# Norm sums and pair sums handed from the vector engine to accumulating transfers in a convolution-and-attention kernel

## The chip, the cores and the metric

The kernel runs on one core of a Trainium2 chip. The metric is the device time of one execution in microseconds, the median of several runs. The core has a matrix engine (PE; its weight loads are listed apart as PEld), a vector engine (DVE), a scalar engine (ACT), a general engine (POOL, also called GpSimd) and a sync engine (SP) that issues most transfers. Each engine works its own list of instructions in order. Sixteen DMA engines move the data of all queues.

## The reference

Four images of 384 channels and 48 x 48 pixels, all in f32. For each image: a 7 x 7 depthwise convolution with a batch norm folded in; a layer norm of the convolution's result over the channels; a layer norm of x; queries, keys and values from the normed x; the normed convolution is added to the queries; attention with 8 heads of 48 over all 2304 pixels; an output projection; and x added at the end.

```python
local = lax.conv_general_dilated(x, conv_w, (1, 1), 'SAME', ..., feature_group_count=C)
local = local * inv[...] + (bn_beta - bn_mean * inv)[...]
x_norm = _layernorm(x_flat, ln_gamma, ln_beta)
q, k, v = split(x_norm @ qkv_w.T + qkv_b)
q = q + _layernorm(local_flat, ln_gamma, ln_beta)
attn = softmax(einsum('bhnd,bhmd->bhnm', q, k) * hd ** -0.5)
out = einsum('bhnm,bhmd->bhnd', attn, v) @ proj_w.T + proj_b
return x_flat + out
```

## The kernel before

Pixels are worked in groups of 8 image rows: G = 384 pixels, NG = 6 groups an image, NT = 24 groups in all. Channels lie on 128 partitions in CC = 3 chunks. Three engines carry the work side by side: PE does all matrix products, ACT the exponentials, and DVE the convolution, one tap of one chunk an instruction (147 steps a group).

**A layer norm** sums over the three chunks on DVE and over partitions by a matmul with a constant matrix:

```python
    class Norm:
        def __init__(self, src):
            self.src = src
            self.buf = work.tile([P, CC, G], F32, tag="sq", name="sq")      # two buffers
        def add(self, src):
            nc.vector.tensor_add(self.buf[:, 0, :], src[:, 0, :], src[:, 1, :])        # L400
            nc.vector.tensor_add(self.buf[:, 0, :], self.buf[:, 0, :], src[:, 2, :])   # L401
        def sum(self):          self.add(self.src)
        def sum_squares(self):  self.add(self.buf)
        def mean(self, m=None):
            self.m = two_banks()[:, 0, :G] if m is None else m
            nc.tensor.matmul(self.m, lhsT=mean_w, rhs=self.buf[:, 0, :], ...)          # L412
        def mean_kept(self):
            m = ring()[:, 0, :G]
            nc.tensor.matmul(m, lhsT=mean_w, rhs=self.buf[:, 0, :], ...)               # L417
            self.m = self.buf[:, 0, :]
            nc.scalar.copy(self.m, m)                                                  # L419
        def root(self, at=slice(0, G)):                      # three steps on ACT, L435 to L437
            nc.scalar.activation(u, self.m[:, at], AF.Ln, bias=eps)
            nc.scalar.activation(y, u, AF.Exp, scale=-0.5)
            nc.scalar.activation(u, y, AF.Square, scale=0.5**0.5)
        # newton() improves the root on DVE; out(), few_centre() ... are the form for later groups,
        # which sums over partitions by transposes and a transfer through DRAM (parts, four)
```

**The prologue** makes keys, values and queries of the first image from x, group after group, and does the first group's convolution beside it:

```python
    first_sum = first_products()
    m, bank = columns()
    convolve_first(10)
    norm = Norm(xn[0, 1])
    norm.sum()
    norm.mean(bank)
    convolve_first(12)
    key_bias(m); query_bias(m)
    next(making)
    norm.centre(); norm.squares()
    # ... (cut)
    for g in range(1, NG):
        last = g == NG - 1
        making = from_x(0, g)
        both(making)
        norm = Norm(accs[0] if last else xn[0, g + 1])
        norm.sum()
        norm.mean()
        if last:
            added = output_bias()         # 18 matmuls of one column, and a copy on ACT
        convolve_first(4)
        norm.centre(); norm.squares()
        both(making)
        # ... (cut)
    query_end(0)
    nc.vector.tensor_add(pb, pb, added)
    plan(n_first - (each - PE_TAPS))
```

**Attention** of one group t takes NSLOT = 12 slots of two halves; a half is three scores. A pair of heads takes three slots, so a pair ends at slots 0, 3, 6 and 9. Scores go to a ring of two PSUM buffers, sums to two more:

```python
    def score(t, p, kb):
        r = ring()
        # ... 8 matmuls into r (L795)
        nc.scalar.activation(pt, r[:, :, :G], AF.Exp, scale=SCALE)     # L803
        weighing.append((t, p, kb, pt))
        if jobs:
            jobs.popleft()()       # one ACT job behind an exponential
    # weigh() does 8 matmuls from pt and the values into sums (L816), two scores later

    def pair_out():
        nc.scalar.copy(dst[0 : 64 + HA], sums[0 : 64 + HA, 0, :G])               # L702
    def pair_add():
        t, p, sums = ended.pop()
        nc.vector.tensor_add(dst, sums[0 : 64 + HA, 1, :G], dst)                 # L711
        # denominators to DRAM (den); after the fourth pair the tails (ao <- aot) too
```

`divide(t - 1)` in slot 2 of the next group loads den, takes reciprocals on DVE and spreads them. The first norm's slots are 8 and 10 for t = 0 (`mean_kept`, then `root`), and 6 and 9 later.

**The plan** gives each half slot a share of convolution steps, from an estimate of the room DVE has in it (`spare`), so that group t + 1 is convolved when its norm begins:

```python
    def spare(t, s, half):
        time = 3.8 - (0.7 if s % 3 == 0 and half else 0.0)    # 0.7 for the pair's add
        # ... less for norms, divisions
```

From the second image on, the keys and values of an image are made before its attention (points "kv"), and the output projection of the image before runs there; it needs `pb`, the output bias.

Of the kernel before, what the change touches and what calls it, by code (L numbers as in the profile page):

```python
# [15 lines left out]
P = 128  # L16
# [29 lines left out]
def unshifted_pass(  # L46
# [55 lines left out]
    def load_packed(dst, src, queue=nc.sync):  # L102
        for p0, piece in segments(src):
            queue.dma_start(out=dst[p0 : p0 + piece.shape[0]], in_=piece)
# [13 lines left out]
    def load_slab(b, g, parts=1):  # L118
        first, end = max(0, g * RG - PAD), min(H, (g + 1) * RG + PAD)
        t = work.tile([P, CC, (RG + 2 * PAD) * W], F32, tag="slab", name=f"slab{b}_{g}")  # L120

        edges = (first, (g + 1) * RG, end) if parts == 2 else (first, end)
        for a, e in zip(edges, edges[1:]):
            load_packed(t[:, :, (a - first) * W : (e - first) * W], x[b, :, a * W : e * W])
        slabs[b, g] = (t, first, end)


    loads = ExitStack()
# [40 lines left out]
                    )  # L169

    load_by_pair(of_ln, ln_pair, (nc.scalar, nc.gpsimd))
    load_slab(0, 0, parts=2)
    place_x(0, 0)
    nc.gpsimd.tensor_scalar_add(inv, norms[:, 3], BN_EPS)
    nc.gpsimd.tensor_tensor(inv, inv, neg_half, ALU.pow)
# [49 lines left out]
        big.tile([P, CC, C], F32, tag=f"k{NG - 1 - i}", name=f"staged{i}") for i in range(3)  # L225
    ]
    load_packed(staged[2], qkv_wT[:, 2 * C :])
    load_packed(staged[1], qkv_wT[:, C : 2 * C])
    load_packed(staged[0], qkv_wT[:, 0:C])
    for g in range(1, NG):  # L230
# [80 lines left out]
    def spare(t, s, half):  # L311
        b, g = divmod(t, NG)
        first, second = norm_slots(t)
        time = 3.8 - (0.7 if s % 3 == 0 and half else 0.0)
        if b + 1 < B and g >= later(b + 1):
            time -= {(3, 1): 2.3, (4, 1): 2.2, (5, 1): 2.3, (7, 0): 0.4, (8, 0): 2.6}.get(
                (s, half), 0.0
            )
        if g:
            time -= {(2, 0): 0.7, (4, 1): 1.4}.get((s, half), 0.0)  # L320
        if t == 0:
            time -= {(7, 1): 1.1, (8, 1): 1.4, (9, 1): 1.1, (11, 0): 5.0}.get((s, half), 0.0)
        elif t + 1 < NT:
            time -= {(5, 1): 2.3, (6, 1): 2.2, (7, 1): 2.3, (9, 0): 0.4, (10, 0): 4.5}.get(
                (s, half), 0.0
            )
        return max(0.3, time)
# [48 lines left out]
    class Norm:  # L376
# [26 lines left out]
        def sum(self):  # L403
            self.add(self.src)

        def sum_squares(self):
            self.add(self.buf)

# [5 lines left out]
        def mean_kept(self):  # L414

            m = ring()[:, 0, :G]
            nc.tensor.matmul(m, lhsT=mean_w, rhs=self.buf[:, 0, :], start=True, stop=True)  # L417
            self.m = self.buf[:, 0, :]
            nc.scalar.copy(self.m, m)  # L419

        def mean_of(self, src, at):

# [8 lines left out]

        def root(self, at=slice(0, G)):

            y, u = self.buf[:, 1, at], self.buf[:, 2, at]
            nc.scalar.activation(u, self.m[:, at], AF.Ln, bias=eps)  # L435
            nc.scalar.activation(y, u, AF.Exp, scale=-0.5)
            nc.scalar.activation(u, y, AF.Square, scale=0.5**0.5)  # L437

        def newton(self, at=slice(0, G)):

# [138 lines left out]
    def both(making):  # L579
        next(making)  # L580
        next(making)
# [72 lines left out]
    def output_bias():  # L654

        m = ring()[:, 0, 0:CC]
        for co in range(CC):
            project(
                m[:, co : co + 1],
                lambda c: w_o[:, c, co * P : (co + 1) * P],  # L660
                lambda c: vbp[:, c, :],
            )
        added = const.tile([P, CC], F32, tag="inv", name="added")
        nc.scalar.copy(added, m)
        return added


    queries = {}
# [21 lines left out]
    def pair_out():  # L690

        if not ended:
            return
        t, p, sums = ended[0]
        if p == 0:
            ao = work.tile([P, CC, G], F32, tag="ao", name=f"ao{t}")
            ao3 = work.tile([P, G], F32, tag="aot", name=f"aot{t}", bufs=1)
            den = dram.tile([NH, G], F32, tag="den", name=f"den{t}")
            outputs[t] = ao, ao3, den
        ao, ao3, den = outputs[t]  # L700
        dst = ao[:, p, :] if p < CC else ao3
        nc.scalar.copy(dst[0 : 64 + HA], sums[0 : 64 + HA, 0, :G])  # L702

    def pair_add():

        if not ended:
            return
        t, p, sums = ended.pop()
        ao, ao3, den = outputs[t]
        dst = (ao[:, p, :] if p < CC else ao3)[0 : 64 + HA]  # L710
        nc.vector.tensor_add(dst, sums[0 : 64 + HA, 1, :G], dst)  # L711
        for j in range(2):
            r = 64 * j
            nc.sync.dma_start(out=den[2 * p + j : 2 * p + j + 1], in_=dst[r + HD : r + HA])
        if p == NP - 1:
            for c in range(CC):
                for r in (0, 64):
                    nc.sync.dma_start(
                        out=ao[r + HD : r + 64, c, :], in_=ao3[r + 16 * c : r + 16 * c + 16]
                    )  # L720
# [105 lines left out]
    def attend(t, s, half):  # L826
# [3 lines left out]
        for kb in range(k0 + n * half, k0 + n * half + n):  # L830
            score(t, p, kb)
            if len(weighing) > LAG:
                weigh()

    def rest():
        while weighing:
            weigh()
        while jobs:
            jobs.popleft()()

# [4 lines left out]
    def convolve_first(n):  # L847
        nonlocal n_first
        n_first += n
        for _ in range(n):  # L850
            next(stream)
# [40 lines left out]
    m, bank = columns()  # L892
    convolve_first(10)
    norm = Norm(xn[0, 1])
    norm.sum()
    norm.mean(bank)
    convolve_first(12)
    key_bias(m)
    query_bias(m)
    next(making)  # L900
    norm.centre()
    norm.squares()
    both(making)
    convolve_first(2)
    add_products()
# [8 lines left out]
    for g in range(1, NG):  # L914

        last = g == NG - 1
        making = from_x(0, g)
        both(making)
        assert not last or n_first >= each - PE_TAPS
        norm = Norm(accs[0] if last else xn[0, g + 1])  # L920
        norm.sum()
        norm.mean()
        if last:
            added = output_bias()
        convolve_first(4)
        norm.centre()
        norm.squares()
        both(making)
        if not last:
            convolve_first(4)  # L930
            both(making)
        norm.sum_squares()
        norm.mean()
        norm.root()
# [3 lines that stand above are left out]
        convolve_first(6 if last else 10)  # L938
        if last:
            local_end(0, norm.newton())  # L940
        else:
            norm.scale(norm.newton())
        both(making)
        if not last:
            convolve_first(7)
    query_end(0)
    nc.vector.tensor_add(pb, pb, added)
    plan(n_first - (each - PE_TAPS))

    for t in range(NT):  # L950
        b, g = divmod(t, NG)
        if g == 0 and b:

            rest()
            pair_out()
            pair_add()
            load_x(b, NG - 1)
            norms_x = {}
            for gk in range(NG):
                before = t - NG + gk  # L960
                load_residual(before)
                making = from_x(b, gk, before, ao if gk < NG - 1 else outputs[before][0])
                new = NG - later(b) + gk if gk < later(b) else None
                old = norms_x.get(gk - 1)
                both(making)
                convolve("kv", t, gk, 0)
                if new is not None:
                    norms_x[gk] = Norm(xn[b, new])
                    norms_x[gk].sum()
                    norms_x[gk].out()  # L970
                both(making)
                if old:
                    old.few_variance()
                    old.few_root()
                if gk == 1:
                    query_end(t)
                    rb = divide(t - 1)
                if gk == 2:
                    last_ao = outputs[t - 1][0]
                    nc.vector.tensor_mul(last_ao, last_ao, rb)  # L980
                convolve("kv", t, gk, 1)
                both(making)
                convolve("kv", t, gk, 2)
                if new is not None:
                    norms_x[gk].few_centre()
                    norms_x[gk].squares()
                both(making)
                convolve("kv", t, gk, 3)
                if old:
                    old.scale(old.few_newton())  # L990
                both(making)
                convolve("kv", t, gk, 4)
                if new is not None:
                    norms_x[gk].sum_squares()
                    norms_x[gk].out()
                both(making)
                if gk < NG - 2:
                    ao = fetch(before + 1)
# [4 lines left out]
        for s in range(NSLOT):  # L1003
# [39 lines left out]
            if coming and s == X_SLOTS[1]:  # L1043
                norm_x.few_root()
            if following and s == second:
                norm.few_root() if t else norm.root()
            if s == first and t == 0:
                norm.centre()
            convolve("slot", t, s, 1)
# [585 lines left out]
```

## Time and profile before

| | |
|---|---|
| time, median of 3 runs | 2857.66 us (2856.81 to 2859.96) |
| profiled span | 2857.6 us |
| prologue | to about 144 us, where the first scores start |
| first image's attention | to about 719 us |
| convolution steps (line 284) | 3447, mean 582 ns by their own records |
| exponentials (line 803) | 1728, 810 ns |
| score matmuls (line 795) and weighing matmuls (line 816) | 13824 each, 8 of each a step |
| pair copies on ACT (line 702), pair adds on DVE (line 711) | 0.47 us, 0.55 us |

In the profile, "L284" is a line of the kernel; a row of the groups or of the order of time names the engine, the operation, what it writes and reads (out<-in), the shapes and how many instructions are merged in it. A bracket at its end tells how long the engine stood idle before it, and what ended that. Durations of overlapping instructions run into each other, so a run of n merged instructions gives a better mean than one record.

### The profile page before, as it was taken

The page shows a single profiled execution, that of the slowest core. Times are in us where ns is not written, and L with a number is a line of the kernel's source. Part 1 is how long each engine was busy: PE and PEld are TensorE (multiplying, and loading weights), DVE is VectorE, ACT ScalarE, POOL GpSimd, SP SyncE. Part 2 cuts the span into 40 slices and gives each one's busy share as a digit, 9 for nine tenths or more (in the row PEclk, how much of TensorE's full clock was granted, in tenths as well). Part 3 has the DMA queues.
Part 4 walks back from the last instruction along what each step waited for, and adds up shares of the span by engine and source line. Part 5 has one row for each costly group of instructions (what it writes and reads, how often), then busy time and mean ns, then how long its engine had stood idle before and what let it go on. Part 6 is the DMA issues. An engine that isn't in the chain of part 4 may idle for free.

```text
span 2857.6 us, 70328 instructions
## 1 busy us (share of the span) xinstructions
PE 2838.7 (99%) x29558; PEld 1778.1 (62%) x29558; DVE 2344.6 (82%) x4635; ACT 1649.5 (58%) x2350; POOL 14.9 (1%) x77
## 2 busy tenths in 40 slices
PE   9999999999999999999999999999999999999999
PEld 5544444654554466666655546888875545788886
DVE  7899999999888988878888889887788787887401
ACT  4366666666226666666622666666652366666662
POOL 1000000000000000000000000000000000000000
PEclk9999999999999999999999999999999999999999
DMA  5101121112231211121132112101113211111111
GB/s 106 40 5 36 45 49 35 36 26 43 71 83 25 46 35 41 31 39 24 38 94 70 28 30 50 36 22 37 44 25 94 53 20 29 43 23 32 46 38 63
DMA packets 103433, 123.71 MB, mean 43 GB/s; under 512 B 43136, under 2 KB 89152, under 8 KB 103104
## 3 DMA queue, kind: packets, MB, share of 16 engines
q1 hardware_dynamic: 99568, 115.48, 17.0%
q8 instruction: 234, 3.83, 0.6%
q10 hardware_dynamic: 2992, 3.62, 0.4%
q14 instruction: 95, 0.78, 0.1%
q0 software_dynamic: 544, 0.01, 0.0%
HBM read 81.39 MB, written 27.03 MB: 38 GB/s over the span
## 4 chain that ended last, share of the span: by engine, by line
PE 92%; DVE 6%; DMA 0%; POOL 0%; ACT 0%; issue 0%; DVEq 0%; ACTq 0%; POOLq 0%
PE o L816 37%; PE r L795 37%; PE o L503 9%; PE r L503 9%; DVE acc L284 5%; DMA pb<-in_proj_b_dram 0%; PE r L299 0%; PE r L412 0%; ACT pt L803 0%; DVE sq L401 0%; DVE xn L681 0%; DMA parts<-part 0%; DVE sq L400 0%; POOL qk_vec L167 0%; DVE acc L672 0%
## 5 line engine op out<-in xcount | busy, mean ns | idle before, releaser
L803 ACT ACTIVATE pt<-r 128x768 f32<-128x768 f32 x1728 | 1399.6, 810 | 760.1 <-PE r L795 743.6
L284 DVE SCALAR_TENSOR_TENSOR acc<-slab,vec,acc 128x368 f32<-128x368 f32 (+6 forms) x3447 | 1756.3, 582 | 1.2
L816 PE MATMUL o<-pt,v 64*64 64x384 f32 x13824 | 1544.7, 483 | 0.0
L795 PE MATMUL r<-xn,k 48*64 48x384 f32 x10368 | 1157.8, 483 | 3.7 <-ACT pt L803 3.7
L816 PEld LDWEIGHTS o<-pt,v 64*64 64x64 f32 x13824 | 715.3, 133 | 406.7 <-issue 224.0
L795 PEld LDWEIGHTS r<-xn,k 48*64 48x64 f32 x10368 | 531.9, 133 | 316.2 <-issue 176.1
L795 PE MATMUL r<-qt,kt 48*64 48x384 f32 x3456 | 388.1, 482 | 0.1
L795 PEld LDWEIGHTS r<-qt,kt 48*64 48x64 f32 x3456 | 181.3, 133 | 99.1 <-issue 43.8
L711 DVE TENSOR_TENSOR ao<-o,ao 113x384 f32<-113x384 f32 x72 | 39.9, 554 | 194.0 <-PE r L795 176.8
L503 PE MATMUL o<-xn,w_qk 128*128 128x384 f32 x450 | 153.3, 486 | 0.0
L503 PE MATMUL r<-xn,w_qk 128*128 128x384 f32 x414 | 141.1, 486 | 0.0
L503 PEld LDWEIGHTS o<-xn,w_qk 128*128 128x128 f32 x450 | 85.5, 190 | 59.6
L503 PEld LDWEIGHTS r<-xn,w_qk 128*128 128x128 f32 x414 | 78.7, 190 | 54.8
L536 ACT COPY v<-r 128x384 f32<-128x384 f32 x42 | 18.2, 482 | 126.9 <-PE r L503 126.9
L503 PE MATMUL r<-w_v,xn 128*128 128x384 f32 x252 | 85.2, 487 | 0.0
L711 DVE TENSOR_TENSOR aot<-o,aot 113x384 f32<-113x384 f32 x24 | 13.3, 556 | 82.4 <-ACT aot L702 64.8
L503 PE MATMUL o<-af,w_o 128*128 128x384 f32 x222 | 75.0, 487 | 0.0
L400 DVE TENSOR_TENSOR sq<-sq 128x384 f32<-128x384 f32 x47 | 26.0, 554 | 57.7 <-ACT sq L395 56.2
L503 PEld LDWEIGHTS r<-w_v,xn 128*128 128x128 f32 x252 | 47.6, 190 | 34.4 <-issue 1.8
L503 PE MATMUL o<-w_v,xn 128*128 128x384 f32 x180 | 64.4, 498 | 1.3 <-ACT w_v L635 1.3
L503 PEld LDWEIGHTS o<-af,w_o 128*128 128x128 f32 x222 | 42.1, 190 | 29.2
L771 DVE SCALAR_TENSOR_TENSOR xr<-r,pb,xr 128x384 f32<-128x384 f32 x27 | 16.4, 617 | 51.8 <-ACT xn L555 41.9
(139 smaller groups left out, 1036.9 us busy)
## 6 DMA issues: line engine op xcount, KB each, us to landing
xr<-in_x_dram SPq DMA_DIRECT2D x24, 576.0 KB
slab<-in_x_dram SPq DMA_DIRECT2D x32, 378.0 KB
held<-ao SPq DMA_DIRECT2D x20, 576.0 KB
af<-held SPq DMA_DIRECT2D x20, 576.0 KB
rb<-rden SPq DMA_DIRECT2D x48, 216.0 KB
out_dram<-xr SPq DMA_DIRECT2D x54, 192.0 KB
xn<-in_x_dram SPq DMA_DIRECT2D x46, 216.0 KB
slab<-in_x_dram SPq DMA_DIRECT2D x14, 297.0 KB
```

The lines of the kernel that those rows point to most:

```text
L284: nc.vector.scalar_tensor_tensor(dst, src, weight, dst, ALU.mult, ALU.add)
L400: nc.vector.tensor_add(self.buf[:, 0, :], src[:, 0, :], src[:, 1, :])
L503: nc.tensor.matmul(dst, lhsT=weights(c), rhs=src(c), start=c == 0, stop=c == CC - 1)
L536: nc.scalar.copy(v[:, blk, :, 0:HD], r[:, :C].rearrange("p (h d) -> p h d", d=HD))
L711: nc.vector.tensor_add(dst, sums[0 : 64 + HA, 1, :G], dst)
L771: nc.vector.scalar_tensor_tensor(xr[:, co, :], m, pb[:, co : co + 1], xr[:, co, :], ALU.add, ALU.add)
L795: nc.tensor.matmul(r[h, j, :G], lhsT=kk[:, blk * P + h.start : blk * P + h.stop], rhs=qq, start=True, stop=True,)
L803: nc.scalar.activation(pt, r[:, :, :G], AF.Exp, scale=SCALE)
L816: nc.tensor.matmul(sums[halves[j], i, :G], lhsT=values[t // NG, kb // NB][h, first : first + 64], rhs=pt[h, j, :], start=kb == 0, stop=kb ...
```

## The change

It takes work off DVE beside the first image. Sums of x over the chunks (groups 1 to 5) are made by three transfers that GpSimd issues: one copy, and two that add to what is there. The two halves of a pair's sums are added in the same way: ACT copies the second half too, and a transfer adds it. The room so made is given to the convolution, in the prologue (14 for 12, 6 for 4 steps) and in the plan. The output bias moves from the last prologue group to the start of the second image. The copy of the first kept mean and the root's three steps become jobs that run one at a time behind exponentials. The first slab's lower rows are loaded after the value weights instead of before them.

```diff
@@ load_slab: two parts, the second loaded by a call
-    load_slab(0, 0, parts=2)
+    rest_of_slab = load_slab(0, 0, parts=2)
@@
     load_packed(staged[2], qkv_wT[:, 2 * C :])
+    rest_of_slab()
     load_packed(staged[1], qkv_wT[:, C : 2 * C])
@@ spare
-        time = 3.8 - (0.7 if s % 3 == 0 and half else 0.0)
+        time = 3.8 - (0.7 if s % 3 == 0 and half and t > NG else 0.0)
@@ Norm
+        def sum_by_transfers(self):
+            nc.gpsimd.dma_start(out=self.buf[:, 0, :], in_=self.src[:, 0, :])
+            for c in (1, 2):
+                nc.gpsimd.dma_start(
+                    out=self.buf[:, 0, :], in_=self.src[:, c, :], accum_op=ALU.add
+                )
@@ mean_kept
-            nc.scalar.copy(self.m, m)
+            jobs.append(lambda: nc.scalar.copy(self.m, m))
@@ root, as three steps that can be queued
+        def root_jobs(self, at=slice(0, G)):
+            y, u, m = self.buf[:, 1, at], self.buf[:, 2, at], self.m[:, at]
+            yield lambda: nc.scalar.activation(u, m, AF.Ln, bias=eps)
+            yield lambda: nc.scalar.activation(y, u, AF.Exp, scale=-0.5)
+            yield lambda: nc.scalar.activation(u, y, AF.Square, scale=0.5**0.5)
@@ output_bias
-        return added
+        nc.vector.tensor_add(pb, pb, added)
@@ pair_out
+        if t < NG:
+            other = work.tile([P, G], F32, tag="other", name="other", bufs=1)
+            def other_half():
+                nc.scalar.copy(other[0 : 64 + HA], sums[0 : 64 + HA, 1, :G])
+                nc.gpsimd.dma_start(
+                    out=dst[0 : 64 + HA], in_=other[0 : 64 + HA], accum_op=ALU.add
+                )
+            jobs.append(other_half)
@@ pair_add
+        all_jobs()
-        nc.vector.tensor_add(dst, sums[0 : 64 + HA, 1, :G], dst)
+        if t >= NG:
+            nc.vector.tensor_add(dst, sums[0 : 64 + HA, 1, :G], dst)
@@ prologue
     norm = Norm(xn[0, 1])
-    norm.sum()
+    norm.sum_by_transfers()
     norm.mean(bank)
-    convolve_first(12)
+    convolve_first(14)
@@
     norm.squares()
+    norm_next = Norm(xn[0, 2])
+    norm_next.sum_by_transfers()
@@ for g in range(1, NG)
-        norm = Norm(accs[0] if last else xn[0, g + 1])
-        norm.sum()
+        if last:
+            norm = Norm(accs[0])
+            norm.sum()
+        else:
+            norm = norm_next
         norm.mean()
-        if last:
-            added = output_bias()
-        convolve_first(4)
+        convolve_first(4 if last else 6)
         norm.centre()
         norm.squares()
+        if g + 2 < NG:
+            norm_next = Norm(xn[0, g + 2])
+            norm_next.sum_by_transfers()
@@
-    nc.vector.tensor_add(pb, pb, added)
@@ start of a later image
+            if b == 1:
+                output_bias()
@@ slots
-                norm.few_root() if t else norm.root()
+                norm.few_root() if t else jobs.extend(norm.root_jobs())
```

More of the change, by code (lines that the diff above doesn't have):

```diff
@@ L120, in load_slab, with load @@
         t = work.tile([P, CC, (RG + 2 * PAD) * W], F32, tag="slab", name=f"slab{b}_{g}")
-        edges = (first, (g + 1) * RG, end) if parts == 2 else (first, end)
-        for a, e in zip(edges, edges[1:]):
+        slabs[b, g] = (t, first, end)
+        def load(a, e):
             load_packed(t[:, :, (a - first) * W : (e - first) * W], x[b, :, a * W : e * W])
-        slabs[b, g] = (t, first, end)
+        if parts == 1:
+            load(first, end)
+        else:
+            load(first, (g + 1) * RG)
+            return lambda: load((g + 1) * RG, end)
     loads = ExitStack()
@@ L432, in root @@
         def root(self, at=slice(0, G)):
[L434 to L437, printed above, removed]
+            for step in self.root_jobs(at):
+                step()
+        def root_jobs(self, at=slice(0, G)):
[3 more added lines that the diff above has]
+            yield lambda: nc.scalar.activation(u, y, AF.Square, scale=0.5**0.5)
         def newton(self, at=slice(0, G)):
@@ L833, in attend, with all_jobs @@
                 weigh()
+    def all_jobs():
+        while jobs:
+            jobs.popleft()()
     def rest():
@@ L837, in rest @@
             weigh()
-        while jobs:
-            jobs.popleft()()
+        all_jobs()
     stream = chain(*(conv_ops(t) for t in range(NT)))
@@ L919, in unshifted_pass @@
         assert not last or n_first >= each - PE_TAPS
-        norm = Norm(accs[0] if last else xn[0, g + 1])
-        norm.sum()
+        if last:
+            norm = Norm(accs[0])
+            norm.sum()
+        else:
+            norm = norm_next
         norm.mean()
-        if last:
-            added = output_bias()
-        convolve_first(4)
+        convolve_first(4 if last else 6)
         norm.centre()
         norm.squares()
+        if g + 2 < NG:
+            norm_next = Norm(xn[0, g + 2])
+            norm_next.sum_by_transfers()
         both(making)
```

## The prediction

> **What bounds the kernel now.** I read the page's busy table first, then PE's own waits, then the table by stage over the first image, then order of time around each gap. The chain by line and the slices added nothing the stages do not show better.
>
> ```profile
> PE 2838.7 (99%) x29558; PEld 1778.1 (62%) x29558; DVE 2344.6 (82%) x4635; ACT 1649.5 (58%) x2350; POOL 14.9 (1%) x77
> ```
>
> PE is busy 2838.7 of 2857.6 us, so all its idle time together is 18.9 us, 0.7% of the span. No change that leaves the matmuls alone can win 2%. What PE waits for, in the view of PE's waits (us in total, times, longest):
>
> ```profile
> PE r L417 <- DVE sq L401: 3.9, 1, 3.9
> PE r L795 <- ACT pt L803: 3.7, 5, 2.6
> ...
> PE r L412 <- DVE sq L401: 1.5, 2, 0.9
> ```
>
> Three gaps after the start-up: one where the mean matmul of the second group's convolution (line 417) waits for a VectorE sum, one where a score waits for an exponential, one at a norm's mean (line 412). The table by stage (length, then busy time of PE, PEld, DVE, ACT, POOL, clock, DMA) says who is behind them:
>
> ```profile
> 150.00:200.00 50.00, 50.00 (x624) 23.47 (x620) 50.00 (x98) 32.03 (x41) 0.00 (x0) 1.00 0.01 2
> 200.00:400.00 200.00, 193.44 (x2312) 92.67 (x2308) 198.00 (x385) 124.62 (x166) 0.00 (x0) 0.97 0.19 43
> ```
>
> Beside the first image DVE is full (50.00 of 50, 198 of 200). ACT has room, POOL does nothing. In order of time around the first gap:
>
> ```profile
> 200.77 11.76 DVE L284 SCALAR_TENSOR_TENSOR acc<-slab,vec,acc 128x368 f32<-128x368 f32 x23
> ...
> 212.45 0.54 DVE L400 TENSOR_TENSOR sq<-acc 128x384 f32<-128x384 f32 x1
> ...
> 213.03 0.56 DVE L401 TENSOR_TENSOR sq<-sq,acc 128x384 f32<-128x384 f32 x1
> ...
> 213.73 1.62 PE L417 MATMUL r<-sq,mean_w 128*128 128x384 f32 x2 [3.93 <-DVE sq L401]
> ...
> 219.18 1.33 PE L816 MATMUL o<-pt,v 64*64 64x384 f32 x8
> ...
> 220.33 0.82 PE L795 MATMUL r<-xn,k 48*64 48x384 f32 x8
> ```
>
> DVE comes 3.93 us late. The gap costs more than itself: groups of eight matmuls start 1.28 us apart until about 220.3, 0.65 after. From 213.73 to 220.33 PE does the mean and four groups, 0.32 + 4 x 0.65 = 2.9 us at full pace, in 6.6: another 3.7. So **gap A is worth 7.6 us**. **Gap B** at 311 us:
>
> ```profile
> 311.07 0.88 PE L795 MATMUL r<-xn,k 48*64 48x384 f32 x8 [2.55 <-ACT pt L803]
> ```
>
> ACT waited for squares whose centring on DVE ended at 309.77; six groups then take 5.62 us instead of 3.88. Worth 2.55 + 1.74 = 4.3. **Gap C** at 125.6 us: 0.92 of wait, then 18 one-column matmuls of the output bias, then six matmuls in 3.45 us instead of 1.94. Worth 0.9 + 1.5 = 2.4. A + B + C = 14.3 us: all three gone would give 2843.4.
>
> **What the Trainium skill says.** "TensorE: Matmul & The Clock Gate", Part 1, says the PE clock halves after an idle window of about 3.4 us and returns after as long a busy one. The trace agrees: the 1.28 and 0.65 us above, and a granted clock of 0.86 in the stretch 200 to 225. "DMA: Bandwidth & Descriptors", SWDGE vs HWDGE vs iDMA, and its Rules for kernel authors: accumulating is for GpSimd-issued transfers alone, and an accumulate must wait for the completion of an earlier transfer to the same bytes. Its Anatomy of one DMA gives about 2.0 us fixed plus bytes / 436 GB/s; for 128 x 384 f32, 197 kB, that is an estimate of 2.45 us each. No accumulate is in this trace, but its GpSimd-issued loads took longer, and much longer while the start-up loads run:
>
> ```profile
> qk_vec<-in_qk_b_dram POOLq DMA_DIRECT2D x2, 1.1 KB, 3.2
> ...
> pb<-in_proj_b_dram POOLq DMA_DIRECT2D x1, 1.5 KB, 7.0
> ```
>
> **The change, part by part.**
>
> *1. Sums of x by transfers.* Five norm sums, two DVE adds each (0.55 + 0.56), leave DVE: 5 x 1.11 = 5.6 us. In exchange 2 + 4 x 2 = 10 more convolution steps are done in the prologue, 10 x 0.52 = 5.2 (the x23 row: 11.76 / 23 = 0.51). DVE's prologue stays as long, but it enters the first image with 20 steps done instead of 10. For groups 2 to 5 the three transfers have a whole group, 18.7 us, to land: hidden. The first does not. Its load is issued from 13.9 us; by the GB/s of the slices up to 60 us about 3.0 MB have moved by 19.5 us and this tile's last byte is near 3.1 MB, so it lands at about 21.5. Its mean is needed when PE reaches it:
>
> ```profile
> 33.46 0.91 PE L412 MATMUL r<-sq,mean_w 128*128 128x384 f32 x2
> ```
>
> That leaves 12 us for three serial transfers. At 4 us each (an estimate: 3.2 measured on small ones and 0.5 to 1 for the bytes) they end at 33.5: no loss. At 7.0 as the pb load had them while all 16 DMA engines were full (DMA stays full to about 38 us), they end at 42.5: PE waits 9 us, and some 1.7 of slow clock follow. PE and DVE both stand, so it is lost whole. I choose +4 as the middle.
>
> *2. Output bias moved to the second image.* 18 matmuls in 2.32 us leave gap C and come back later: zero by themselves. The slow 1.5 us after them should go; some of the 0.9 may. PE then gets to the mean of the squares earlier, and DVE's 2.45 us wait for the root at 136.7 closes. -2.
>
> *3. Pair halves by copy and transfer.* Four DVE adds a group leave, 4 x 0.55 = 2.2 us, 24 x 0.554 = 13.3 us in the image. ACT gets 24 copies of 0.47, each behind an exponential, in a pause of 0.48: they fit. The transfer itself is read only by the reciprocals: copies at 250.5 and about 252, transfer 4 to 256, denominators 2, then SP issues six tail transfers in 3.7 and the reload of den at about 262, landing near 265. The reciprocal ran at 267.12 and DVE will be some us earlier: 0 to 2 us of DVE wait per group, 0 on PE.
>
> *4. The plan.* Working the plan's formula through with the new room: up to the point before the mean of gap A 131 steps instead of 137, and up to slot 6 of the second group 274 instead of 284. **Gap A**: DVE saves 6 x 0.52 + 2 x 0.54 + 0.1 = 4.3 us there; part 2 makes PE about 1.4 us more early than DVE. Lateness 3.93 + 1.4 - 4.3 = about 1 us, too short for the clock to fall. -7.6 + 1 = -6.6. **Gap B**: between A and B DVE saves 4 more steps and 4 adds, 4.2, but PE comes 3.7 earlier because the slow clock of A is gone, and part 5 costs DVE some 2.5. It stays about as it is: 0.
>
> *5. Steps behind exponentials.* The kept mean takes one of two ring buffers. Its copy moves from straight after the mean to after the next exponential (233.38 mean, next exponential 235.22 to 236.03): the second score, which started at 235.57 and takes the buffer the mean had, now starts at about 236.55. 1 us, at slots 8 and 10: +2. The root's three steps (0.61, 0.53, 0.52) now end near 243.0, after the third exponential of slot 11, instead of 240.24. DVE stood 0.60 for them and will stand up to 3.
>
> *6. Rest of the first slab behind the value weights.* Weights come about 1.2 us earlier (216 kB at 180 GB/s), but PE then waits for the last weights at 19.75 anyway, whose place in the queue is unchanged: 0.
>
> Sum: +4 - 2 - 6.6 + 0 + 2 + 0 = -2.6; 2857.66 - 2.6 = 2855.1. Since parts 1 and 5 are costs that I inferred and part 4 is a gain that the trace shows directly, I lean a little towards the gain: **2854.5 us**.
>
> **The rivals.** *The first sum becomes the new wait.* For it: three dependent transfers, full DMA engines, 7.0 us for 1.5 KB, PE in order. Against: a packet of another queue need not wait behind all that is outstanding; 3.2 was measured at 8 us. With 10.7 in place of 4: about 2861. *The start is hidden and gap B closes too.* For it: DVE loses 13.3 us of adds in an image where it is full; against: the faster PE eats it between A and B. Then -2 - 6.6 - 4.3 + 2: about 2847. *Transfers of 113 rows are slow*, the denominators come late and DVE stalls in each of five groups. For it: 113 rows do not divide over 16 engines. Against: the 12 to 15 us that lie between. At 5 us more each, DVE falls behind PE again and gap A's saving is lost at B: about 2863.
>
> **Range and chances.** The two outcomes of part 1 lie near 2848 and 2860, with a few us of spread from B and C on each side; the three runs of before spread by 3. Eight in ten: 2845 to 2866. A gain of 2% needs 57 us where 18.9 exist; a loss of 2% needs a repeated stall nowhere seen. Faster 0.005, within 2% 0.985, slower 0.01.
>
> **What would show it.** Part 1: PE's wait before the mean at about 33 us, named for a transfer into sq; 0 to 1 us says hidden, over 5 says the rival. Parts 3 and 4: no wait over 1.5 us at the kept mean near 210, clock 1.00 there, DVE adds of ao only from the second image on. B: a wait of some 2 to 3 us for an exponential near 300; none says DVE gained more than I think. Part 5: two gaps of about 1 us before the second score after each kept mean. Part 2: no slow matmuls at 128, perhaps some near 715. Wrong outright would be waits in later images, where DVE has slack.

## The result, and the profile after

The changed kernel takes 2870.15 us (median of 4 runs, 2869.6 to 2871.37) against 2858.14 us of the kernel before in the same comparison: a ratio of 1.0042, 95% interval 1.0025 to 1.006. It is 12 us slower, and outside the predicted range of 2845 to 2866.

The busy table of the kernel after:

```profile
PE 2837.4 (99%) x29558; PEld 1872.0 (65%) x29558; DVE 2328.5 (81%) x4601; ACT 1658.9 (58%) x2374; POOL 46.4 (2%) x116
```

DVE lost 16 us of work, as meant, and PE does the same matmuls. But PE's idle time rose from 18.9 us to 2869.5 - 2837.4 = 32.1. PE's waits of the kernel after (us in total, times, longest) say where:

```profile
PE r L427 <- DMA sq<-xn: 14.4, 1, 14.4
PE r L828 <- ACT pt L836: 5.2, 7, 3.4
...
PE r L427 <- DVE sq L408: 0.5, 1, 0.5
```

The 3.9 us for the first kept mean's sum is gone. In its place stands one wait of 14.4 us for a transfer into sq: the chain of three transfers that makes the first sum. The wait for an exponential has grown from 2.6 to 3.4. The stages of the kernel after, in the columns shown before:

```profile
0.00:50.00 50.00, 31.37 (x161) 22.86 (x162) 21.87 (x65) 19.84 (x61) 15.74 (x46) 0.88 0.98 162
...
150.00:200.00 50.00, 49.71 (x550) 24.83 (x552) 49.93 (x96) 30.32 (x41) 0.88 (x1) 1.00 0.06 10
200.00:400.00 200.00, 195.72 (x2360) 96.65 (x2355) 195.51 (x379) 129.56 (x177) 6.67 (x8) 0.98 0.23 47
```

In the first 50 us PE is busy for 31.37 (44.99 before), and the DMA engines are busy for 98% of the stretch. From 200 to 400 us PE is busy 2.3 us longer than before, in spite of its wait at 318 us. The chain itself, in the kernel after's order of time from 18 us on:

```profile
23.69 0.55 POOL L415 DMA_DIRECT2D sq<-xn  x1 [9.53 <-DMA xn<-in_x_dram]
...
31.75 0.91 POOL L417 DMA_DIRECT2D sq<-xn  x1 [7.51 <-DMA sq<-xn]
...
38.87 0.87 POOL L417 DMA_DIRECT2D sq<-xn  x1 [6.20 <-DMA sq<-xn]
...
48.15 1.65 PE L427 MATMUL r<-sq,mean_w 128*128 128x384 f32 x2 [14.42 <-DMA sq<-xn]
...
49.83 0.16 DVE L670 TENSOR_TENSOR qkb<-qk_vec,r 128x3 f32<-128x3 f32 x1 [15.98 <-PE r L427]
```

Each bracket names what the engine waited for: in the first row GpSimd (POOL) waits for the load of x, in the next two for its own transfer before. The three take about 8, 7 and 9 us, one after the other; PE reaches the mean at 33.7 us, 0.3 later than before, and stands until 48.15. DVE stands 15.98 us with it, so nothing is done in that time that was saved elsewhere. Later sums run the same three transfers in 3.0 us each (a median). The transfers into sq in the stretches 20 to 50 us and 50 to 140 us (count, KB each, median us to landing):

```profile
sq<-xn POOLq DMA_DIRECT2D x5, 192.0 KB, 7.8
```

```profile
sq<-xn POOLq DMA_DIRECT2D x10, 192.0 KB, 3.0
```

The two gaps of the first image, in the kernel after's order of time:

```profile
221.54 0.85 PE L849 MATMUL o<-pt,v 64*64 64x384 f32 x8
222.32 0.91 PE L432 MATMUL r<-sq,mean_w 128*128 128x384 f32 x2
223.16 0.88 PE L828 MATMUL r<-xn,k 48*64 48x384 f32 x8
223.86 0.83 PE L849 MATMUL o<-pt,v 64*64 64x384 f32 x8
225.03 0.88 PE L828 MATMUL r<-xn,k 48*64 48x384 f32 x8 [0.34 <-ACT pt L836]
...
318.63 1.56 PE L828 MATMUL r<-xn,k 48*64 48x384 f32 x8 [3.39 <-ACT pt L836]
```

Gap A is closed: the mean follows the matmuls before it and the clock stays full. The score at 225.03 comes 1.17 us after the group before it, not 0.65. It takes the buffer that the mean had, and the copy out of that buffer now stands behind an exponential (224.16 us) and starts at 224.87. Gap B is wider. Six points that both profiles have, as starts of the same instruction, make a ledger:

| point | before | after | difference | step |
|---|---|---|---|---|
| first mean of the prologue | 33.46 | 48.15 | +14.7 | |
| second mean | 38.80 | 54.38 | +15.6 | +0.9: 1.45 of slow clock after the wait, less a wait of 0.56 that is gone |
| first score | 144.35 | 156.93 | +12.6 | -3.0, of which 2.3 is the bias, moved |
| second kept mean (slot 10) | 233.38 | 239.41 | +6.0 | -6.6, gap A |
| first score of the second group's last pair | 320.57 | 329.33 | +8.8 | +2.7, gap B |
| first score of the second image | 857.82 | 868.52 | +10.7 | +1.9, the bias |

From there to the last matmul the difference stays 10.7; the last 1.2 of the span's 11.9 come behind it, in the last output transfers, which the change doesn't touch.

### The profile page after: what moved, and what is told of

Its sections match the earlier page's. It is cut to its first block, busy times and chain, and to the rows that moved or that the text cites. A ratio compares the mean times of both kernels' runs of the same rounds, so it can differ in the third digit from the quotient of the medians.

```text
span 2869.5 us, 70442 instructions
## 1 busy us (share of the span) xinstructions
PE 2837.4 (99%) x29558; PEld 1872.0 (65%) x29558; DVE 2328.5 (81%) x4601; ACT 1658.9 (58%) x2374; POOL 46.4 (2%) x116
## 3 DMA queue, kind: packets, MB, share of 16 engines
q10 hardware_dynamic: 2992, 3.62, 0.4%
## 4 chain that ended last, share of the span: by engine, by line
PE 94%; DVE 4%; DMA 1%; issue 1%; ACT 0%; SPq 0%; POOL 0%; DVEq 0%; POOLq 0%; ACTq 0%
PE r L828 38%; PE o L849 38%; PE o L522 9%; PE r L522 9%; DVE acc L291 3%; DMA staged<-in_qkv_wT_dram 0%; DMA sq<-xn 0%; DMA xn<-in_x_dram 0%; ACT pt L836 0%; PE r L427 0%; DVE xn L517 0%; DMA parts<-part 0%; DMA slab<-in_x_dram 0%; DVE xn L443 0%; DVE sq L461 0%
## 5 line engine op out<-in xcount | busy, mean ns | idle before, releaser
L849 PE MATMUL o<-pt,v 64*64 64x384 f32 x13824 | 1575.9, 483 | 0.0
L828 PE MATMUL r<-xn,k 48*64 48x384 f32 x10368 | 1179.9, 483 | 5.1 <-ACT pt L836 4.9
L849 PEld LDWEIGHTS o<-pt,v 64*64 64x64 f32 x13824 | 763.8, 133 | 359.3 <-issue 143.6
L828 PEld LDWEIGHTS r<-xn,k 48*64 48x64 f32 x10368 | 566.6, 133 | 282.9 <-issue 111.0
L828 PE MATMUL r<-qt,kt 48*64 48x384 f32 x3456 | 397.1, 482 | 0.3 <-ACT pt L836 0.3
L828 PEld LDWEIGHTS r<-qt,kt 48*64 48x64 f32 x3456 | 194.4, 133 | 86.8 <-issue 29.1
L744 DVE TENSOR_TENSOR ao<-o,ao 113x384 f32<-113x384 f32 x54 | 30.0, 556 | 194.7 <-PE r L828 176.6
```

The lines of the kernel that those rows point to most:

```text
L828: nc.tensor.matmul(r[h, j, :G], lhsT=kk[:, blk * P + h.start : blk * P + h.stop], rhs=qq, start=True, stop=True,)
L849: nc.tensor.matmul(sums[halves[j], i, :G], lhsT=values[t // NG, kb // NB][h, first : first + 64], rhs=pt[h, j, :], start=kb == 0, stop=kb ...
```

## The experiments

My theory: the chain of the first sum costs the 15.6 us, because the DMA engines are full of start-up loads; without it the change is a gain. The rivals: something else would make PE wait there anyway; an accumulating transfer is slow at the start by itself; and what the deferred copies win or lose was open. Every time below is a median beside runs of the kernel before on the same chip.

**The first sum on DVE again**, all else as changed:

```diff
     norm = Norm(xn[0, 1])
-    norm.sum_by_transfers()
+    norm.sum()
     norm.mean(bank)
```

> The changed kernel with the sum of group 1 alone made by two vector adds again, all else as changed. Theory (the three chained transfers of the first sum, beside the start-up loads, cost the 14.4 us wait and about 1 us of slow clock after it): the wait at the first mean goes to 0 to 1 us and the time falls by 14 to 16 us to 2854 to 2857. Rival (the transfers only show a wait that something else, such as the later arrival of loads, would bring anyway): the wait stays above 5 us and the time above 2861.

Measured: 2855.05 us, ratio 0.9988 (0.9981 to 0.9995). PE's wait for a transfer into sq is gone from its list; the first score starts at 141.50 us. The one line turns a loss of 12 us into a gain of 3.5. **The chain alone**, in the kernel before:

```diff
     norm = Norm(xn[0, 1])
-    norm.sum()
+    norm.sum_by_transfers()
     norm.mean(bank)
```

> The kernel before with the sum of group 1 alone made by three transfers, and nothing else of the change. Theory: the same wait of 13 to 16 us appears before the first mean, and the time rises by 13 to 17 us to 2871 to 2875. Rival (the wait needs the other parts, such as the next group's transfers that go out behind the third one, or the moved slab rows): a wait under 8 us and a time under 2867.

Measured: 2875.08 us, ratio 1.0053 (1.0036 to 1.007), 16.5 us over the kernel before, at the upper end of what was expected. PE's waits in it:

```profile
PE r L420 <- DMA sq<-xn: 14.0, 1, 14.0
PE r L425 <- DVE sq L401: 3.9, 1, 3.9
```

The same wait without any other part of the change, and gap A still there. So the chain is cause enough, both ways.

**Why it is slow.** All else as changed, but the loads that stand behind x's group 1 are issued later, by ACT, group by group:

```diff
-    for g in range(1, NG):
-        load_x(0, g)
+    load_x(0, 1)
-    load_packed(w_o, proj_wT)
@@ prologue
+    load_x(0, 2, nc.scalar)
     first_sum = first_products()
@@ after norm.squares()
+    load_x(0, 3, nc.scalar)
@@ in the loop over g, after norm.squares(): load_x(0, g + 3), the second slab at g == 1, w_o at g == 3
```

> The changed kernel with the loads of x of groups 2 to 5, of the second slab and of the projection weights issued later, by ACT, one group at a time, so that the three transfers of the first sum run while little else moves. Theory (each transfer is slow because the DMA engines are full of loads): each takes 3 to 4 us instead of 7 to 9, the wait at the first mean falls to 0 to 2 us, the time to 2854 to 2859. Rival (an accumulating transfer is slow at the start by itself, or GpSimd is slow to issue it): each still takes 6 us or more, and the wait stays above 7 us.

Measured: 2856.14 us, ratio 0.999 (0.9983 to 0.9996). The order of time of this kernel:

```profile
22.52 0.55 POOL L415 DMA_DIRECT2D sq<-xn  x1 [9.01 <-DMA xn<-in_x_dram]
...
27.04 0.91 POOL L417 DMA_DIRECT2D sq<-xn  x1 [3.97 <-DMA sq<-xn]
...
32.16 0.87 POOL L417 DMA_DIRECT2D sq<-xn  x1 [4.21 <-DMA sq<-xn]
...
35.30 1.65 PE L427 MATMUL r<-sq,mean_w 128*128 128x384 f32 x2 [2.06 <-DMA sq<-xn]
```

4.5, 5.1 and 3.1 us instead of 8, 7 and 9, with the same instructions at the same place. While these three run, the DMA engines are busy for 0.55, 0.71 and 0.55 of the time; in the changed kernel for 0.99 or more. The first two missed the 3 to 4 us expected: a load of 1.2 MB for residuals (SP at 16.5 us) and the next group's (ACT at 26.4 us) still run beside them. The wait falls from 14.4 to 2.06. It is the load on the DMA engines; neither the accumulate nor GpSimd's issue is slow by itself. Nor does DVE's work hold GpSimd up: in the changed kernel the third transfer took 9.28 us while DVE stood still.

**Copy and root straight in ACT's order**, all else as changed:

```diff
-            jobs.append(lambda: nc.scalar.copy(self.m, m))
+            nc.scalar.copy(self.m, m)
@@
-                norm.few_root() if t else jobs.extend(norm.root_jobs())
+                norm.few_root() if t else norm.root()
```

> The changed kernel with the copy of the kept mean and the three root steps straight in ACT's order again instead of behind exponentials. Theory (the copy behind an exponential holds one of two ring buffers and makes a gap of about 1.1 us twice): both gaps go, and 2 to 4 us are won, 2866 to 2868. Rival (the jobs shield PE from ACT, as they were meant to): no gain, or up to 3 us more.

Measured: 2865.05 us, ratio 1.0024 (1.0016 to 1.0033), 5 us under the changed kernel. That is more than expected, but not all of it belongs to the edit: in this profile the first mean waits 12.4 us, 2 less than in the changed kernel, since x's group 1 landed 1.7 us earlier. From the first score on (154.62) to the second group's last pair (321.19) it takes 166.6 us, against 172.4 in the changed kernel: the edit is worth 5.8 us there. Gap B went from 3.39 us to 1.68, and the slow clock behind it is gone (six groups took 6.81 us from 318.63 in the changed kernel, 3.88 at full pace: 2.9 of the 5.8):

```profile
313.37 0.88 PE L828 MATMUL r<-xn,k 48*64 48x384 f32 x8 [1.68 <-ACT pt L836]
```

**Both remedies together**, and the first sum made by PE, which needs no vector work at all:

```diff
     norm = Norm(xn[0, 1])
-    norm.sum_by_transfers()
-    norm.mean(bank)
+    norm.m = bank
+    project(bank, lambda c: mean_w, lambda c: norm.src[:, c, :])
```

> The changed kernel with the sum of group 1 made by PE (three accumulating matmuls into the mean instead of one) and the kept mean's copy and the root straight in ACT's order. Theory (the first sum costs some 15 us, the two deferrals some 5 us, and the two add up): 2849 to 2852, a ratio to the kernel before of 0.997 to 0.998. Rival (the direct copies won only because they took time out of what the long wait had shifted): no better than the kernel with the sum on the vector engine alone, 2854 to 2856.

Measured: 2851.48 us, ratio 0.9975 (0.9965 to 0.9984). The profiled span is 2848.6. This beats both kernels, the one before by 7 to 8 us. What PE waits for in it between 150 and 860 us is one row:

```profile
PE r L828 <- ACT pt L836: 2.0, 2, 1.7
```

From this kernel I took single parts out again. **Which of the two deferrals** costs: the root deferred alone, then the copies alone.

```diff
-                norm.few_root() if t else norm.root()
+                norm.few_root() if t else jobs.extend(norm.root_jobs())
```

> The kernel with the sum on PE and the kept mean's copy direct, but the root's three steps behind exponentials as in the change. Theory (the later root makes the vector engine stand about 2.6 us for it, and what it loses comes out at the gap near 300 us): that wait grows from 1.7 to 3 us or more, with slow clock after it, and the time is 2 to 4 us above the kernel with both direct. Rival (the whole loss of the deferrals is the mean's copy): within 1 us of it.

Measured: 2855.8 us, ratio 0.9991 (0.9983 to 0.9999). DVE's and PE's rows in the order of time:

```profile
234.38 0.62 DVE L461 SCALAR_TENSOR_TENSOR sq<-sq,eps 128x384 f32<-128x384 f32 x1 [1.45 <-ACT sq L456]
```

```profile
303.73 0.88 PE L828 MATMUL r<-xn,k 48*64 48x384 f32 x8 [3.62 <-ACT pt L836]
```

Without the deferral DVE's step starts at 232.16 us, with no wait. With 1.45 us of standing at 234, gap B at 304 grows from 1.68 to 3.62 us. From the first score to the second group's last pair it takes 2.0 us more than with both direct (168.55 for 166.54); no slow clock followed this time. The median is 4.3 us higher; what this profile has beyond the 2.0 lies elsewhere (its scores start 0.7 us later, and 1.7 us of slow matmuls come at 711 us), and is not shown to be the edit's.

```diff
-            nc.scalar.copy(self.m, m)
+            jobs.append(lambda: nc.scalar.copy(self.m, m))
```

> The kernel with the sum on PE and the root direct, but the copies of the kept mean behind an exponential as in the change. Theory (each copy holds one of the two ring buffers for one exponential longer): two gaps of about 1.1 us at slots 8 and 10 of the first group, the time about 2 us above the kernel with both direct, the gap near 300 us at about 1 us or less because PE comes later to it. Rival (the copy is harmless): within 1 us and no gaps.

Measured: 2852.62 us, ratio 0.9978 (0.9969 to 0.9988), not to be told from the kernel with both direct. Its gaps are there, half as long as expected, and gap B is shorter for them:

```profile
210.47 0.88 PE L828 MATMUL r<-xn,k 48*64 48x384 f32 x8 [0.34 <-ACT pt L836]
...
227.57 0.88 PE L828 MATMUL r<-qt,kt 48*64 48x384 f32 x8 [0.34 <-ACT pt L836]
...
301.60 0.88 PE L828 MATMUL r<-xn,k 48*64 48x384 f32 x8 [1.03 <-ACT pt L836]
```

By the same two points it takes 0.5 us more (167.03). So of the two the root is the costly one; with the slow clock that such a gap B can bring, the parts make up 5.4 of the 5.8: 2.0 + 0.5 + 2.9. **The pair halves on DVE again:**

```diff
-        time = 3.8 - (0.7 if s % 3 == 0 and half and t > NG else 0.0)
+        time = 3.8 - (0.7 if s % 3 == 0 and half else 0.0)
@@ pair_out
-        if t < NG:
+        if t < 0:
@@ pair_add
-        if t >= NG:
+        if t >= 0:
```

> The same, and the pair halves of the first image added by the vector engine again, with the plan's room as before. It tells what the pair transfers bring. Theory (the 13 us of vector work they take away matter only up to the gaps near 205 and 300 us, where the vector engine is late): PE waits 1 to 3 us longer there, the time is 2 to 5 us more than without this edit. Rival (the ten convolution steps done in the prologue are enough by themselves): within 1 us of it.

Measured: 2854.59 us, ratio 0.9985 (0.9978 to 0.9991). Gap B is 3.2 us, and 0.3 us of wait stand at the second kept mean (225.09 us); gap A stays closed. From PE's waits and from the order of time:

```profile
PE r L432 <- DVE sq L408: 0.3, 1, 0.3
```

```profile
303.38 0.88 PE L828 MATMUL r<-xn,k 48*64 48x384 f32 x8 [3.20 <-ACT pt L836]
```

The pair transfers bring about 3 us. **The sums of groups 2 to 5 on DVE again**, with 12 and 4 steps in the prologue:

```diff
-    convolve_first(14)
+    convolve_first(12)
@@
-            norm = norm_next
+        norm = Norm(accs[0] if last else xn[0, g + 1])
+        norm.sum()
@@
-        convolve_first(4 if last else 6)
+        convolve_first(4)
@@ norm_next and the calls that start its transfers are gone
```

> The kernel with the sum of group 1 on PE and the direct copies, and the sums of groups 2 to 5 by vector adds as before, with 12 and 4 convolution steps in the prologue as before. It tells what the hidden transfers of sums bring. Theory (ten steps fewer are done when the first image starts, 5 us of vector work): a wait of 1 to 4 us comes back at the kept mean near 205 us or the one near 300 grows, and the time is 2 to 6 us more. Rival (the pair transfers alone are enough): within 1 us.

Measured: 2858.58 us, ratio 1.0 (0.9992 to 1.0009). Gap A is back, with its slow clock:

```profile
211.93 1.62 PE L432 MATMUL r<-sq,mean_w 128*128 128x384 f32 x2 [2.95 <-DVE sq L408]
```

The hidden sums by transfer, with the ten steps they make room for, bring about 7 us, more than expected and more than the pairs. With the 3 us of the pairs that is more than the whole gain over the kernel before, so the two are not a sum; a kernel without both was not run. Last, **more of the same**, 8 steps for 6 in each of four prologue groups:

```diff
-        convolve_first(4 if last else 6)
+        convolve_first(4 if last else 8)
```

> The kernel with the sum on PE and the direct copies, and 8 instead of 6 convolution steps in each of the four prologue groups, so 8 steps (4.2 us of vector work) fewer are left for the first image. Theory (the gap near 300 us comes from a vector engine that is late by 2 us or so): that wait goes from about 1.7 us to under 0.5 and 1 to 3 us are won, 2847 to 2850. Rival (the vector engine is full in the prologue too): PE waits there by as much, and nothing is won.

Measured: 2851.87 us, ratio 0.9974 (0.9966 to 0.9983): nothing won. Gap B is gone (0.3 us is all PE waits for an exponential from 150 to 860 us), but the first score starts at 144.34 us instead of 142.31. The rival holds: DVE is full in the prologue too, and what gap B gave the prologue took.

## Why the prediction was wrong, step by step

**Part 1 failed, by the size that I chose.** "I choose +4 as the middle" between 0 and 10.7; measured +15.6 (14.4 of wait, 0.3 of shift, and 0.9 that the slow clock cost beyond a wait of 0.56 that went away). Three terms were off, all one way. The tile was used from 23.69 us on, not 21.5. The transfers took 8, 7 and 9 us instead of 7.0 each at most, since they lengthen the load they stand in: before, the DMA engines were full to about 38 us; in the kernel after, to about 47. And the argument against, that "a packet of another queue need not wait behind all that is outstanding", did not help: the first transfer landed by 31.75 us, with the engines full to about 47, but sharing them was slow enough; with the load taken away the same three took 12.8 us instead of 24.5. I had a measured 7.0 us for a transfer of 1.5 KB (issued at 12.15 us) beside the same start-up loads and set an estimate of 4 from idle engines beside it as equally likely. With the 7.0 believed, the rival's number, 2861, would have been the prediction, and still 9 us short.

**Part 1's other half was right**: in the loop the sums are hidden (no PE wait for one), and ten steps enter the first image early. Taking it out cost 7 us.

**Part 2** was close: -3.0 at the first score and +1.9 in the second image are -1.1 where I had -2; a wait of 1.0 us at 146.4 for an ACT copy took its place. The slow clock after the bias matmuls went from 128 us; see below for where it can come back.

**Part 3** was right: the copies fit behind exponentials (0.47 us, no wait of PE named for them), and up to 860 us DVE waited for the reloaded denominators once, 1.5 us. The rival of slow 113-row transfers has nothing for it.

**Part 4** was right on gap A: it closed, -6.6 predicted, -6.6 measured. That the figures agree is luck. From the group before the mean to the fifth group behind it the kernel before takes 11.36 us (208.97 to 220.33), the kernel after 4.83 (221.54 to 226.37), of which 0.52 are a gap of part 5: so gap A was worth 7.05, not 7.6 (mean and next start are 0.84 apart at full pace, where I had put 0.32). DVE came in time, where I had left 1 us of lateness, and the 0.52 made up the rest. On gap B it was not: 0 predicted, +2.7 with the second such gap in it, so +2.2. Gap B is now worth 3.39 + 2.93 = 6.3 us, against 4.3: the wait is 0.8 longer, where I had the root's 2.5 us of DVE (2.64 measured, at 249.50) balanced by other savings, and 1.2 more is slow clock, which I had left at its old size.

**Part 5** had the right mechanism for the copies at twice the size: 1.17 - 0.65 = 0.52 us each, +1.0 instead of +2. The root's delay to DVE, which the same part names, is what gap B shows. The score starts at 225.03, while the copy's record runs from 224.87 to 225.34; why it can start before that ends was not tried.

**Part 6** was right: the weights are used earlier and PE waits longer for the last ones (1.85 us for 0.93), to 19.95 us where it was 19.75.

Sum by the ledger: +15.6 - 1.1 - 6.6 + 2.7 = +10.6, and 1.2 behind the last matmul: 11.8 of the 12.0. The kernel with the first sum on PE and the direct copies shows what the rest of the reasoning was worth: 2851.5, with gap A closed and gap B at 1.7.

## What to carry to other kernels

A transfer takes longer in company: the same 192 KB took 7 to 9 us beside the start-up loads and 3.0 later. Before handing a sum on the critical path to transfers, take its latency from rows of the same stretch of the profile, with the same engines busy, and multiply by the length of the chain. Work moved off a full engine pays only up to the next point where that engine is late, so name that point and count what reaches it; here 13 us of adds taken away were worth 3. A step put behind other work to shield one engine delays its reader: look at who reads it, here DVE, and how late that one is already.

## What the runs showed that I had not expected

The clock can fall behind one-column matmuls. The 18 bias matmuls take some 2.2 us in which PE counts as busy, yet in four of ten profiles of kernels that have them in the second image the twelve matmuls behind them take 5.81 us instead of 4.12. In the kernel with the deferred copies and in the one with both direct:

```profile
706.99 2.17 PE L522 MATMUL r<-vbp,w_o 128*128 128x1 f32 x18
709.02 5.81 PE L522 MATMUL r<-w_v,xn 128*128 128x384 f32 x12
```

```profile
706.43 2.17 PE L522 MATMUL r<-vbp,w_o 128*128 128x1 f32 x18
708.46 4.12 PE L522 MATMUL r<-w_v,xn 128*128 128x384 f32 x12
```

The Trainium skill, "TensorE: Matmul & The Clock Gate", Part 1, says that the window in which activity is judged runs free; that fits a cost of 1.7 us that comes in some profiles and not in others, and in the kernel before it came at 128 us. That the low activity of one column is what trips it was not tried by itself. Nor does the length of a gap alone decide, against the idle window of about 3.4 us on which the prediction went: matmuls at half pace followed gaps of 2.55 us (gap B of the kernel before) and 2.95 (the last but one experiment), and none followed the 3.62 with the root deferred. A slow clock that comes and goes also means that differences of 1 to 2 us between single profiles here are not differences of kernels.
